# A depthwise convolution of the last pair of images on TensorE instead of VectorE, and some products of the late scans on GpSimd

## The chip, the cores and the metric

The kernel runs on one core of a Trainium2 chip. A core has five engines that run side by side, each through its own fixed list of instructions: TensorE (PE in the profile, with its weight loads shown apart as PEld), VectorE (DVE), ScalarE (ACT), GpSimd (POOL) and SyncE (SP), which here only issues DMA transfers. Operands lie in SBUF, and matmul results in the eight banks of PSUM. The metric is the device time of one execution in microseconds, given as the median of several runs.

## The reference

A network of two layers on x of shape (8, 256, 32, 32) in float32, that is eight images of 1024 tokens with 256 channels. Cut to what matters:

```python
# layer 0: a selective state space block, then a mixture of experts
h  = layernorm_over_channels(x)                     # (B, L=1024, 256)
xs, z = split(h @ W_in)                             # 512 channels each
xs = silu(causal_conv4(xs) + conv_b)
dt, Bm, Cm = parts(xs @ W_x)                        # dt through W_dt and softplus
for t in range(L):                                  # 16 states per channel
    hst = exp(dt[t] * A) * hst + dt[t] * xs[t] * Bm[t]
    y[t] = sum_over_states(hst * Cm[t])
x = x + ((y + xs * Dp) * silu(z)) @ W_out
x = x + sum over the 2 best of 8 experts of p_e * (gelu(x @ W1_e + b1_e) @ W2_e + b2_e)

# layer 1: an inception-like convolution, then a feed-forward of chosen tokens
v = layernorm_over_channels(x)                      # 256 channels in five parts:
#   128 unchanged | 32: 3x3 depthwise | 32: 1x11 depthwise | 32: 11x1 depthwise
#   | 32: a small state space block (64 channels, 16 states), as in layer 0
x = x + concat(parts)
w = layernorm(x) @ wr                               # rank the tokens of an image
x = x + feed_forward(256 -> 1024 -> 256, tanh-gelu) for the 511 best of 1024 tokens
```

## The kernel before

**Units and groups.** Layer 0's state space block is done in 16 *units*, each half an image (512 tokens). A unit has `norm`, `project`, `rows_of`, `dt_of` and `scan_unit`; the scans are 2 channel blocks x 8 pairs of states x 2 halves of the block, called *scan pairs* (two states at once). What follows is done in four *groups*, a pair of images each (n = 0 to 3; "pair 3" is the last): `route`, `scatter` with `put` (tokens go to slots of experts by indirect DMA), `experts` (23 blocks of 128 slots or fewer), `combine` (the outputs of the experts are gathered into the buffers `ys` and weighted), `taps_of` (the depthwise convolutions), `mamba_in`, `mamba_scan`, `mamba_out`, `assemble`, `ranks`, a second `put`, `feed_forward` in eight halves, and `finish`.

**One scan pair** (`scan_pair`), with the lines of the profile: GpSimd writes `dbu` = dtx * B for two states (line 801, 128 x 1024); ScalarE writes exp(dt * A) to a PSUM bank of the pool `mm` (line 806, once for each state); VectorE scans along the tokens, writing the states over that bank (line 809), and multiplies them by C, writing over `dbu` (line 812). TensorE then sums over the states by multiplying with an identity matrix into the PSUM tile `y` (as transposes in the units, line 793; as matmuls of 512 columns in the groups, line 830). In some pairs GpSimd first adds the two products (line 820), and TensorE has one summand instead of two. `PAIRED[i]` says for how many of the eight pairs of states of unit or group i this is so. When the state of a first half is needed by the second, a ScalarE copy keeps it (line 816). `end_y` closes a scan with a VectorE product of `y` with the gate (line 876). There are six `dbu` buffers, and four late in the kernel.

**The depthwise convolutions** (`taps_of`) of a pair of images read two padded images in SBUF, `pad_a` (128 partitions: the 3x3 and the 1x11 parts of both images, 17 shifts) and `pad_b` (64 partitions: the 11x1 part, 11 shifts). The first shift of each is a ScalarE instruction with scale and bias (line 1406), every other one a VectorE multiply-and-add of 1024 columns with one scale per partition (line 1408), on an accumulator in SBUF. So there are 28 shifts or *taps* for each pair of images, 26 of them on VectorE.

**The small state space block.** `mamba_in` turns the tokens (VectorE transposes of line 1422), projects and convolves them (TensorE, line 1462) and makes delta and dtx (line 773); `mamba_scan` has 8 pairs of states x 2 images = 16 scan pairs.

**The rest that is spoken of.** In `experts` and `feed_forward` the matmuls are those of lines 1219 (`hidden`) and 1241 (`second`). `combine` gathers by GpSimd's indirect DMA into two `ys` buffers (line 1317) and weighs by VectorE (lines 1335 and 1338). `ranks` counts by VectorE how many tokens of an image rank above each (lines 1618, 1623 and 1629). `put` is an indirect DMA too (line 1130), as is the gather of `finish` (line 1705). Line 1322 makes small diagonal matrices on ScalarE.

**The order.** No engine chooses at run time. Every piece of work is a `step` with an engine, an estimate of its duration, a priority and the buffers it reads and writes; `Flow.run` simulates the engines with these estimates and writes down one fixed order for each of them. The priorities come from a plan written by hand or tuned: `UNIT_AT` (when the scans of each unit begin), `PLAN` (one row for each group: where each of its parts begins, and the spacing of its pieces), and `KNOB` (how the choice weighs waits and buffers). For the matmuls of 128 x 512 in float32 that sum in the groups the steps say 0.9 us:

```python
step(PE, (0.48 if turned else 0.9) * (1 if paired else 2), prio + 2.5, sums, [dbu], [y], scan=True)
```

## Time and profile before

| | |
|---|---|
| median of 3 runs | 3333.59 us (3333.14 to 3346.01) |
| the profiled execution, its own time | 3336.01 us |
| its span in the profile | 3334.2 us |
| mean granted TensorE clock | 0.958 of full speed |
| TensorE busy | 2939.6 us (88%), weight loads 2009.1 us (60%) |
| VectorE busy | 2833.6 us (85%) |
| ScalarE busy | 2317.7 us (70%) |
| GpSimd busy | 2298.9 us (69%) |
| mean DMA rate | 203 GB/s |

The span is what the profile's timeline covers; the rest of the execution's own time lies around it. Busy shares are means over stages with different limits: up to 2452 us the units and the groups of earlier pairs are interleaved, after that the last pair of images goes through its parts one after another, with the remaining work of pair 2 beside it. A row of the groups of instructions reads: line, engine, operation, output <- inputs, shapes, count, then total busy us and the mean ns of one, then the idle time of the engine just before these instructions, and what ended most of it.

### The profile page before, as it was taken

How to read it: one execution, taken by the hardware profiler on the slowest of the kernel's cores; microseconds unless marked ns; L12 is line 12 of the kernel's file. 1: busy time of each engine (PE TensorE's matmuls, PEld its weight loads, DVE VectorE, ACT ScalarE, POOL GpSimd, SP SyncE). 2: the span in 40 equal slices, each digit the busy share in tenths (PEclk: the TensorE clock that was granted, in tenths of full speed). 3: DMA queues.
4: the chain of work that ended last, by engine and by line, in shares of the span. 5: the costliest groups of instructions: out<-in, count | busy, mean ns of one | idle time of the engine just before them, and what ended most of it. 6: DMA issues, size and time to landing. Idle time of an engine off the chain costs nothing. (4 is left out here: it accounts for less than half of the span.)

```text
span 3334.2 us, 43327 instructions
## 1 busy us (share of the span) xinstructions
PE 2939.6 (88%) x13348; PEld 2009.1 (60%) x13348; DVE 2833.6 (85%) x3924; ACT 2317.7 (70%) x4290; POOL 2298.9 (69%) x1650
## 2 busy tenths in 40 slices
PE   8888887888898989999999999898898889989948
PEld 4454554555656666666676664666766557865636
DVE  3999999999989998999998998968997889768841
ACT  5566776567878878988877876777856666557523
POOL 4678677688899969887776886785728764166331
PEclk9998999899999999999999999999998999999979
DMA  7343443345646556765555776666748787877745
GB/s 253 135 148 130 139 140 131 123 159 181 217 161 210 183 193 223 244 201 174 192 198 185 234 234 228 204 209 208 237 150 306 253 316 270 264 261 263 242 160 160
DMA packets 276709, 676.99 MB, mean 203 GB/s; under 512 B 31015, under 2 KB 115629, under 8 KB 276478
## 3 DMA queue, kind: packets, MB, share of 16 engines
q1 hardware_dynamic: 258046, 623.87, 56.0%
q0 software_dynamic: 18432, 50.36, 4.6%
q8 instruction: 107, 1.75, 0.2%
q14 instruction: 124, 1.02, 0.1%
HBM read 572.92 MB, written 101.19 MB: 202 GB/s over the span
## 5 line engine op out<-in xcount | busy, mean ns | idle before, releaser
L801 POOL TENSOR_TENSOR dbu<-dtx,bc 128x1024 f32<-128x1024 f32 x547 | 1291.2, 2375 | 236.2 <-DMA bc<-rows 109.2
L806 ACT ACTIVATE mm<-dt,neg_a 128x512 f32<-128x512 f32 x1152 | 771.3, 688 | 138.8 <-DVE dbu L812 121.8
L812 DVE TENSOR_TENSOR dbu<-mm,bc 128x512 f32<-128x512 f32 x1108 | 765.4, 691 | 50.7 <-DMA bc<-rows 1.4
L809 DVE TENSOR_TENSOR_SCAN mm<-mm,dbu 128x512 f32<-128x512 f32 x566 | 691.6, 1222 | 95.5 <-ACT mm L806 53.1
L809 DVE TENSOR_TENSOR_SCAN mm<-mm,state,dbu 128x512 f32<-128x512 f32 x562 | 720.7, 1282 | 21.8 <-ACT mm L806 15.3
L793 PE MATMUL y<-ident,dbu 128*128 128x128 f32 x3768 | 547.4, 286 | 183.6 <-DVE dbu L812 95.2
L793 PEld LDWEIGHTS y<-ident,dbu 128*128 128x128 f32 x3768 | 444.7, 146 | 367.8 <-POOL dbu L820 115.7
L1219 PE MATMUL mm<-xbt,we 128*128 128x256 f32 x1584 | 378.0, 390 | 11.3 <-ACT xbt L1207 3.5
L1241 PE MATMUL mm<-we,hid 128*128 128x256 f32 x1552 | 368.6, 387 | 13.3 <-ACT hid L1225 7.0
L1219 PEld LDWEIGHTS mm<-xbt,we 128*128 128x128 f32 x1584 | 304.2, 196 | 69.4 <-issue 10.6
L1241 PEld LDWEIGHTS mm<-we,hid 128*128 128x128 f32 x1552 | 290.1, 193 | 80.5 <-issue 20.6
L820 POOL TENSOR_TENSOR dbu<-dbu 128x512 f32<-128x512 f32 x174 | 227.0, 1305 | 119.4 <-DVE dbu L812 109.8
L816 ACT COPY state<-mm 128x1 f32<-128x1 f32 x576 | 90.0, 159 | 282.4 <-DVE dbu L812 272.6
L534 PE MATMUL y<-still 128*128 128x512 bf16 x1062 | 278.7, 397 | 0.0
L436 ACT ACT_TABLE_LOAD x198 | 254.0, 1283 | 3.7
L728 PE MATMUL mm<-pre,w_tap 128*128 128x512 f32 (+3 forms) x512 | 233.8, 598 | 7.2 <-ACT pre L716 6.0
L1225 ACT ACTIVATE hid<-mm,we 128x256 f32<-128x256 f32 x396 | 157.2, 475 | 35.5 <-PE mm L1219 20.1
L534 PEld LDWEIGHTS <-still 128*128 128x128 bf16 x1062 | 107.5, 102 | 110.5 <-issue 32.2
L1317 POOL DMA_INDIRECT ys<-slots_y,slot x128 | 127.1, 993 | 63.8 <-issue 26.0
L1705 POOL DMA_INDIRECT ys<-y,slot_t x64 | 64.8, 1013 | 153.7 <-DMA y<-xo 74.2
L728 PEld LDWEIGHTS mm<-pre,w_tap 128*128 128x128 f32 x512 | 92.4, 189 | 110.7 <-issue 93.9
L1130 POOL DMA_INDIRECT slots_x<-xg,slot x116 | 115.7, 997 | 39.9 <-issue 22.1
(289 smaller groups left out, 4661.4 us busy)
## 6 DMA issues: line engine op xcount, KB each, us to landing
bc<-rows SPq DMA_DIRECT2D x606, 512.0 KB
we<-in_W SPq DMA_DIRECT2D x81, 514.0 KB
we<-in_W SPq DMA_DIRECT2D x76, 512.0 KB
xb<-slots_x SPq DMA_DIRECT2D x92, 256.0 KB
slots_y<-xo SPq DMA_DIRECT2D x92, 256.0 KB
xc<-x SPq DMA_DIRECT2D x64, 256.0 KB
we<-in_W12f SPq DMA_DIRECT2D x21, 512.0 KB
slots_x<-xg SPq DMA_DIRECT2D x10, 1024.0 KB
```

The source lines that it names most:

```text
L436: nc.scalar.preload_act_table_set(tables[name])
L534: nc.tensor.matmul(live[0].v[:, 0], still, wide, start=False, stop=False)
L728: nc.tensor.matmul(tc_.v[:, cut:], w_tap[:, c, j], pre.v[:, cut + j : j + N], start=j == 3, stop=j == 0)
L793: nc.tensor.matmul(y.v[:, n, k * P : (k + 1) * P], src[:, k * P : (k + 1) * P], g.ident, start=start and k == 0, stop=stop and k == N // P ...
L801: gpsimd(2.38, prio, lambda: nc.gpsimd.tensor_tensor(dbu.v, dtxs.v[:, n : n + 1].to_broadcast(wide2), bt.v, ALU.mult), [dtxs, bt], [dbu], ...
L806: step(ACT, 0.69, prio, lambda j=j, h=h: nc.scalar.activation(h.v, dts.v[:, n], AF.Exp, scale=scales(j)), [dts], [h], table="exp", scan=True)
L809: step(DVE, 1.29 if at else 1.24, prio, lambda j=j, h=h: nc.vector.tensor_tensor_scan(h.v, h.v, dbu.v[:, j], 0.0 if initial is None else i ...
L812: product = step(DVE, 0.69, prio, lambda j=j, h=h: nc.vector.tensor_tensor(dbu.v[:, j], h.v, ct.v[:, j], ALU.mult), [h, ct], [dbu], scan=True)
L820: gpsimd(1.27, prio + 2.3, lambda: nc.gpsimd.tensor_tensor(dbu.v[:, 0], dbu.v[:, 0], dbu.v[:, 1], ALU.add), [], [dbu])
L1219: nc.tensor.matmul(tv[:, f], we[0].v[:, at : at + P], xbt.v[:, k], start=k == 0, stop=k == KC - 1)
L1225: nc.scalar.activation(hid.v[:, f], tv[:, f % 2], func, bias=we[0].v[:, at : at + 1])
L1241: nc.tensor.matmul(to, hid.v[:, f, h * P : (h + 1) * P], we[1].v[:, f * C : (f + 1) * C], start=extra is None and f == 0, stop=f == FC - 1,)
```

## The change

1. `taps_of` of pair 3 (n at or above `PE_TAPS` = 3) becomes TensorE work: every tap is a matmul with a diagonal matrix that holds the tap's weights, two halves of 512 columns each, summed in a PSUM bank (17 matmuls a half for `pad_a`, 11 for `pad_b`, 56 in all), in steps of four matmuls. ScalarE adds the bias and moves each half to the accumulator (4 instructions). The 26 VectorE and 2 ScalarE tap instructions of pair 3 are gone; pairs 0 to 2 keep theirs.
2. The 28 diagonal matrices are made by ScalarE (`spread_taps`, identity scaled per partition) in the SBUF places of the weights `w_pre`, `w_z` and `w_tap`, after the last `project` of layer 0 has read them.
3. A third kind of scan pair (`way` 2, a new list `HELD`): the scan writes the states over `dbu` in SBUF instead of over the PSUM bank, and GpSimd multiplies both by C in one instruction of 128 x 1024; TensorE sums two summands. It is used for 1 of 16 scan pairs in the small block of pair 1, 2 of 16 of pair 2, and 8 of 16 of pair 3.
4. `PAIRED` has other numbers: 180 added pairs in the units instead of 140, 24 in the groups instead of 38.
5. `UNIT_AT`, `PLAN` and `KNOB` have other numbers, so that the order of the other work moves too.

VectorE has 26 taps (104 to 78) and 22 products by C (1152 to 1130) less; GpSimd has 11 products by C more and 204 added pairs instead of 178. The number of transfers that SyncE issues is the same.

```diff
-PAIRED = [0, 3, 0, 2, 0, 0, 7, 6, 4, 0, 1, 0, 0, 5, 4, 3, 5, 5, 7, 2]
+PAIRED = [0, 4, 6, 4, 0, 1, 7, 2, 0, 2, 2, 0, 2, 5, 5, 5, 5, 1, 7, 1]
+HELD = [0, 0, 0, 0, 0, 0, 0, 0, 0, 0, 0, 0, 0, 0, 0, 0, 0, 1, 2, 8]
-UNIT_AT = [13, 52, 84, 119, 151, 183, 212, 243, 272, 303, 335, 367, 399, 430, 484, 522]
+UNIT_AT = [13, 56, 87, 118, 150, 183, 212, 242, 273, 304, 335, 367, 399, 430, 484, 522]
 PLAN = [
...
-    dict(put=4.35, experts=(475.48, 5.13), combine=(531.8, 1.84), taps=(660.36, 4.99), mamba=607.2, assemble=(658.29, 21.36), ranks=726.99, ffn=(887.16, 13.4), finish=(1263.31, 3.88)),
-    dict(put=8.79, experts=(589.95, 1), combine=(560.3, 13.52), taps=(748.92, 14.82), mamba=705.93, assemble=(727.02, 4.16), ranks=770.82, ffn=(1019.15, 1.97), finish=(1226.33, 0.05)),
+    dict(put=5.38, experts=(475.47, 5.12), combine=(521.25, 1.33), taps=(808.33, 6.52), mamba=613.73, assemble=(682.87, 25.29), ranks=744.51, ffn=(960.78, 5.51), finish=(1163.97, 13.06)),
+    dict(put=6.66, experts=(606.01, 1.74), combine=(783.79, 8.25), taps=(813.44, 7.71), mamba=683.76, assemble=(688.24, 0.97), ranks=770.96, ffn=(997.48, 5.59), finish=(1332.62, 0.63)),
 ]
+PE_TAPS = 3
-KNOB = [0.35, 0.14, 0.68, 0.65, 0, 1.38, 562.08]
+KNOB = [0.35, 0.13, 0.66, 0.63, 0, 1.4, 437.89]
...
+    def way_of(i, k):
+        def share(n, k, of):
+            return (k + 1) * n // of > k * n // of
+        return 2 if share(HELD[i], k, DS) else 1 if share(PAIRED[i], k // 2, DS // 2) else 0
...
+            step(DVE, us, prio, lambda j=j, h=h: nc.vector.tensor_tensor_scan(
+                dbu.v[:, j], h.v, dbu.v[:, j], 0.0 if initial is None else initial[1](j), ALU.mult, ALU.add),
+                [h, *at], [dbu], scan=True, ways=(2,))
...
+        if last is not None:
+            step(ACT, 0.17, prio + 1, lambda: nc.scalar.copy(
+                last[2](), dbu.v[:, :, N - 1 :]), [dbu], fills=[last[0]], ways=(2,))
+        gpsimd(2.38, prio + 1, lambda: nc.gpsimd.tensor_tensor(
+            dbu.v, dbu.v, ct.v, ALU.mult), [ct], [dbu], ways=(2,))
...
+    def tap_matrices():
+        places = [w_pre[:, k, c * P : (c + 1) * P] for k in range(KC) for c in range(NC0)]
+        places += [w_z[:, k, c * P : (c + 1) * P] for k in range(KC) for c in range(NC0)]
+        places += [w_tap[:, c, j] for c in range(NC0) for j in range(4)]
+        return [places[: len(TAPS_A)], places[len(TAPS_A) : len(TAPS_A) + len(TAPS_B)]]
...
+    def spread_taps(prio):
+        made = buf("token")
+        diagonals.append(made)
+        for k, (taps, scale, m) in enumerate([(TAPS_A, taps_a, P), (TAPS_B, taps_b, DI1)]):
+            for i in range(len(taps)):
+                step(ACT, 0.3, prio + 0.1 * i, lambda k=k, i=i, scale=scale, m=m: nc.scalar.activation(
+                    tap_matrices()[k][i][:m, :m], g.ident[:m, :m], AF.Copy, scale=scale[:, i : i + 1]),
+                    fills=[made]).needs.update(projections)
...
+            for hf in range(2 if n >= PE_TAPS else 0):
+                (t,) = banks()
+                for first in range(0, len(taps), 4):
+                    some = range(first, min(first + 4, len(taps)))
+                    now = prio + each * (first + hf + k * len(TAPS_A))
+                    def go(some=some, t=t, k=k, m=m, taps=taps, hf=hf, window=window):
+                        for i in some:
+                            nc.tensor.matmul(
+                                t.v[:m].rearrange("p (h w) -> p h w", w=32), tap_matrices()[k][i][:m, :m],
+                                window(*taps[i], top=16 * hf, high=16), start=i == 0, stop=i == len(taps) - 1,
+                            )
+                    step(PE, 0.45 * len(some), now, go, [at, *diagonals], [t], claims=[acc])
+                step(ACT, 0.62, prio + each * (len(taps) + hf + k * len(TAPS_A)), lambda t=t, acc=acc, scale=scale, m=m, taps=taps, hf=hf:
+                    nc.scalar.activation(
+                        acc.v[:m, 16 * hf : 16 * hf + 16], t.v[:m].rearrange("p (h w) -> p h w", w=32), AF.Identity,
+                        bias=scale[:, len(taps) :]), [t], fills=[acc])
...
         end = s + 2 * DS
         tokens(i, end + 1)
+        if i + 1 == len(units):
+            spread_taps(end + 2)
```

## The prediction, made before the changed kernel had run

> **What bounds the kernel now.** I read the page first, then stretches cut at the kernel's own joints, then the timelines of the joints.
>
> ```profile
> span 3334.2 us, 43327 instructions
> PE 2939.6 (88%) x13348; PEld 2009.1 (60%) x13348; DVE 2833.6 (85%) x3924; ACT 2317.7 (70%) x4290; POOL 2298.9 (69%) x1650
> ```
>
> No engine is full over the span, so the stages decide. The sixteen units of layer 0 end with the VectorE product of line 876 at 2452. Until then (busy shares between one such product and the next) VectorE is 84 to 97% busy in nearly every half unit. After it comes one long chain for the last pair of images (pair 3): route, scatter, experts, combine, convolution and mamba, assembly, ranks, feed-forward, finish. The stretches of that chain, with columns PE, PEld, DVE, ACT, POOL (busy us), granted clock, DMA share, GB/s:
>
> ```profile
> 2452.00:2691.00 239.00, 212.26 (x806) 140.57 (x804) 195.75 (x368) 147.28 (x282) 158.28 (x172) 0.92 0.72 240
> 2809.00:2921.00 112.00, 110.61 (x565) 95.38 (x564) 87.84 (x272) 53.15 (x117) 13.23 (x24) 1.00 0.78 247
> 2921.00:3005.00 84.00, 68.70 (x303) 49.72 (x302) 50.75 (x170) 45.99 (x94) 52.95 (x69) 0.95 0.80 262
> 3005.00:3053.00 48.00, 45.24 (x157) 24.48 (x155) 39.35 (x30) 37.74 (x59) 30.47 (x24) 0.98 0.68 227
> 3053.00:3129.00 76.00, 67.14 (x230) 41.07 (x231) 74.69 (x79) 46.72 (x86) 46.97 (x26) 0.93 0.83 290
> 3129.00:3204.00 75.00, 50.19 (x245) 37.86 (x243) 56.99 (x218) 23.51 (x50) 5.85 (x6) 0.87 0.42 134
> ```
>
> The reader should see four limits: 2809 to 2921 belongs to TensorE (experts, 110.6 of 112 us); 2921 to 3005 (combine of pair 3) to no engine; 3053 to 3129 (scans of pair 3) to VectorE (74.7 of 76); what follows is serial. In the combine stage it is a ring of gathers through two ys buffers, as the waits from 2460 to 3010 show:
>
> ```profile
> POOL ys L1317 <- DVE xo L1338: 20.5, 14, 5.2
> DVE xo L1338 <- DMA ys<-slots_y,slot: 17.8, 14, 3.2
> DVE xo L1335 <- DMA ys<-slots_y,slot: 16.2, 10, 3.9
> ```
>
> Eight blocks take 2936.9 to 3000.8, 8 us each, with VectorE at 60%. The timelines around the start of the last scans:
>
> ```profile
> 3018.98 15.80 DVE L1408 SCALAR_TENSOR_TENSOR dbu<-pad_a,taps_a,dbu 128x1024 f32<-128x1024 f32 x12
> 3039.97 13.24 DVE L1408 SCALAR_TENSOR_TENSOR dbu<-pad_b,taps_b,dbu 64x1024 f32<-64x1024 f32 x4
> 3053.14 1.21 DVE L809 TENSOR_TENSOR_SCAN mm<-mm,dbu 128x512 f32<-128x512 f32 x1
> 3042.35 3.21 POOL L773 TENSOR_TENSOR dtx<-dt,xs 128x1024 f32<-128x1024 f32 x1
> 3016.71 7.14 PE L1462 MATMUL mm<-xn,w_tap 64*128 64x512 f32 x16 [0.21 <-DVE xn L1447]
> ```
>
> Two thirds of the taps run while mamba_in(3) is still on its way to the first scan (3005 to 3048): VectorE would be idle there. And four taps take 13.24 us beside GpSimd, 3.31 each, against 1.32 (15.80/12) without.
>
> **The change part by part.** (1) Off VectorE for pair 3: 26 taps. By the rows above 16 cost 1.3 and ten cost 1.3 to 3.3, together 43 us. Of these only what stands in the scan stage is on the path: B taps until 3053.1, where the first dbu was ready at 3048.8 (4.3 us), two between scans (1.95 + 1.27), and those at 3125.8, which mostly wait beside GpSimd and the end anyway. So 7 to 10 us of 43, unless other work moves into the vacated 3005 to 3048. It does: in the new order both rank passes of pair 2 (36 us, from 2907 on before, the second among the first combine blocks) stand between mamba_in(3) and the first scan. The first pass came from a stretch where TensorE was the limit (110.6 of 112), so moving it gains nothing there; the second held up combine: its first product came at 2936.9, though its gathers were issued at 2926.9 to 2931.7 and take some 3 us to land. I take 4 us there, and 1 us for pair 2's puts no longer between the gathers; bounds 0 and 12. The ring of 8 us a block stays.
>
> (2) On TensorE: 28 taps x 2 halves = 56 matmuls of 512 columns. The nearest row is line 1462: 16 records are 8 such matmuls in 7.14 us, 0.89 each; taken at 0.87 for long runs, 49 us. The Trainium skill (TensorE: Matmul & The Clock Gate, section "Wait — 56ns, not 53.3ns?") gives warm matmuls a spacing of N/2.4 GHz plus about 2.5 ns, 0.216 us for 512 columns; with two records to a matmul the 56 would take 24 us, close to the 0.45 us each that the new step declares. The row has 0.446 us for one record, twice that, in f32. The measured one decides: 25 us more on TensorE than the order was laid out for. It matters, since only in this stage does TensorE get this work: in the order, 20 matmuls stand before the first sums of y and 36 among them. They also hold two of the mm banks at a time, which feed-forward would use; its two halves there are the ones that wait.
>
> (3) The scan stage of pair 3 summed by engine. T is the transpose of line 1422 (3004.9); before, the first scan is at T+48.2 and the product of line 876 that closes the stage at T+124.5. After: GpSimd's three leading products fall from 3.0-3.2 to 2.4 without taps beside them (-2), B taps no longer precede the first scan (-4), four tap matmuls stand ahead of the second delta matmul (+1.5, net of a feed-forward pass that stood there before): first scan near T+44. VectorE from there: 8 ordinary pairs x (2x1.25+2x0.69) + 8 held x 2x1.28 + 4 of other work = 55 us, so T+99. GpSimd from T+40: 16x2.36 + 8x2.36 held + an add 1.3 + puts and gathers 6 = 64, so T+105. TensorE: in order, behind the second delta matmul (T+31): 48 tap matmuls still to come 42, sums of y 31x0.87 = 27, two feed-forward halves (16 matmuls each, 7.1 by lines 1219 and 1241) and small ones 17: 86 us, so T+117, plus 2 to 4 for waits on sums and for the tap results holding two of the dbu buffers: T+119 to T+121. TensorE replaces VectorE as the limit here; gain about 4 us instead of 20. Five feed-forward halves of group 2 left this stage (35 us), or it would be longer.
>
> (4) Held C products. No row has a scan writing SBUF. From below: 1.22, as the PSUM form; from above 3.3, if it were blocked like the taps. The skill (SBUF — State Buffer, "Who interferes with whom") says a VectorE instruction with at most one SBUF input does not contend with GpSimd, and one with two does. This scan reads h from PSUM and dbu from SBUF, like the present one, whose mean is 1.22 to 1.28 beside a GpSimd that is 69% busy. I take 1.28; at 3.3 it would be 22x2 = +44 on VectorE. For the product on GpSimd I take line 801's 2.36, same shape; bounds 2.34 and 3.3. It waits for both scans of its pair; queued behind it in GpSimd's order are the dbu products of the pairs after next and puts of pair 2, and TensorE's sums wait for it, 2.4 us later than for a VectorE product. One or two dbu products run ahead of it in the order, so scans do not see it unless GpSimd is the limit.
>
> (5) Matrices: 28 ACT copies; nearest row line 1322, 0.39 us: 11 us during unit 15, where ACT is 73% busy and only the exps of the scans queue behind. Zero; uncovered at most 11, and 3 is what I keep for the range. State copies fall by a handful. SP issues as many DMAs as before.
>
> (6) PAIRED: 204 instead of 178 adds of 1.3 us; in the units 180 instead of 140: +52 us GpSimd, and 160 transposes fewer, -17 us TensorE. Unit 2 gets 24 (31 us): its GpSimd share goes from 0.65-0.78 to 0.9-0.97; units 7 to 9 lose 32. Half units with GpSimd at 0.88 or more had VectorE at 0.91 in the mean, the others before 2002 at 0.94: 2 us of 65 each. By GpSimd's work in the new order some ten half units are so crowded, nine before. Net 0, bounds -8 and +10.
>
> (7) Tail. All eight feed-forward halves of pair 2 now stand behind the last scan, four before: 28 us more TensorE in 3129 to 3204 and the next stretch, where it has 25 + 17 idle. GpSimd's puts for pair 3 still start behind one gather of pair 2, which needs the product behind ranks, as before (ranks end 3203.7, put 3209.8). So 0, bounds -5 and +8; 28 if TensorE's cover were gone.
>
> Sum: 0 (units) -5 (until T) -4 (scans) +0 (tail) = -9 on the profiled execution's 3336.0, hence 3327; the median of the runs shown is 2.4 lower, and I forecast 3326.
>
> **The rivals.** *Full gain:* the VectorE time is worth its length: 42 us of taps and 15 of products (22x0.69) come off a chain that was VectorE-bound. For it: 74.7 of 76 us. Against it: only 16 of these pairs' stage is so bound. Needs TensorE to keep pace; then T+105 rather than T+120, and with 10 us in the combine it gives -25 to -40: about 3303. *Slower, by TensorE in the last scans:* the sums of y stand behind eight-matmul tap groups (7 us each), the dbu buffers are freed late, GpSimd waits for them, scans wait for it. Price: at the granted 0.93 of that stretch 86 us become 92, and a wait of 2.5 us at each of eight pairs adds 20: T+142, and feed-forward of pair 2 is pushed into ranks and puts for another 5 to 10. +10 to +30: about 3352. It decides once the last sum comes later than T+125. *Not doing what it says:* that the order moves nothing off the path (ranks fill every gap, combine's ring stays at 8 us): -2 to +5, part of the likeliest.
>
> **How the numbers follow.** Likeliest case 0.43 (own range 3310 to 3340), full gain 0.34, slower 0.23. A measurement here can tell about 0.5% (17 us) from no change. Below 3317: 0.31 of the full gain and 0.09 of the likeliest: 0.40. Above 3350: 0.20 of the slower case and 0.02 of the likeliest: 0.22. Between: 0.38. Range 3296 to 3356, leaving out a tenth at either end: the full gain with its last 10 us of combine, and the slower case beyond its middle.
>
> **What would show it.** Line 1454's matmuls at 0.43 per record (0.21 would favour the full gain); the scan stage with PE at 95% and VectorE under 80%; first scan at T+44, last product near T+120; combine still 8 us a block; line 820's scans at 1.2 to 1.3; a GpSimd-crowded unit 2. I am wrong if T itself moves by more than 12 us, if the units' end moves from 2452 by more than 10, or if the last scans end before T+110 or after T+130.

## The result and the profile after

The changed kernel takes 3366.09 us (median of 8 runs, 3360.15 to 3374.7) against 3342.05 us for the kernel before (8 runs, 3333.14 to 3352.21, the three shown ahead among them): a ratio of 1.0074, 95% interval 1.0057 to 1.0092. It is slower by about 24 us where some 9 us less had been forecast. The page of the profiled execution:

```profile
span 3365.0 us, 43189 instructions
...
PE 2980.5 (89%) x13300; PEld 2024.6 (60%) x13300; DVE 2775.1 (82%) x3876; ACT 2309.9 (69%) x4312; POOL 2345.8 (70%) x1693
```

Against the page before, VectorE has 58.5 us less (2775.1 against 2833.6), GpSimd 46.9 more, TensorE 40.9 more, and the span is 30.8 longer. So VectorE was relieved as planned, and the kernel still became slower. The same stretches of the changed kernel, cut at the same events (columns PE, PEld, DVE, ACT, POOL busy us, granted clock, DMA share, GB/s):

```profile
2470.00:2714.00 244.00, 213.46 (x824) 141.25 (x822) 199.27 (x373) 146.98 (x283) 150.10 (x168) 0.95 0.72 240
...
2852.00:2944.00 92.00, 87.86 (x434) 74.86 (x433) 67.47 (x183) 37.91 (x86) 13.31 (x24) 0.98 0.67 214
2944.00:3024.00 80.00, 66.46 (x290) 48.89 (x288) 39.39 (x119) 45.66 (x97) 44.54 (x58) 0.94 0.83 270
3024.00:3069.00 45.00, 44.86 (x139) 21.50 (x138) 40.80 (x144) 25.15 (x39) 12.90 (x8) 1.00 0.41 136
3069.00:3145.00 76.00, 75.47 (x213) 34.66 (x212) 56.47 (x57) 36.88 (x75) 59.19 (x32) 1.00 0.70 225
3145.00:3231.00 86.00, 72.85 (x328) 51.14 (x327) 55.24 (x214) 30.82 (x63) 18.81 (x29) 0.94 0.66 210
```

The stage of the last scans (3069 to 3145) has TensorE at 75.5 of 76 us and VectorE at 56.5; before (the row 3053 to 3129 of the prediction) it was 67.1 and 74.7. The stretch ahead of it (3024 to 3069) is a TensorE stretch too, and VectorE is busy there for 40.8 of 45 us, mostly with pair 2's ranks. Set side by side, with T the first transpose of mamba_in(3):

| stretch, from the two profiled executions | before | after | difference |
|---|---|---|---|
| start to the last unit's gate product | 2452.4 | 2470.4 | +18.0 |
| units' end to T | 552.5 | 553.9 | +1.4 |
| T to the first scan of pair 3 | 48.2 | 45.2 | -3.0 |
| first scan to the gate product that closes the stage | 76.3 | 75.9 | -0.4 |
| that product to the end of ranks(3) | 74.3 | 85.9 | +11.6 |
| ranks(3) to the end | 130.5 | 133.7 | +3.2 |
| sum | 3334.2 | 3365.0 | +30.8 |

The profiled execution before was among the fastest of its kernel, so these differences add up to nearly 7 more than the medians show. The middle, where the change sits, is as forecast. The loss is at both ends, in work that the taps and the held scans hardly touch: 18 us in the units and 15 in the tail.

**The units.** VectorE's totals until the units' end, before and then after:

```profile
0.00:2453.70 2453.70, 2181.04 (x10196) 1474.71 (x10196) 2204.89 (x2603) 1829.55 (x3351) 1878.88 (x1235) 0.97 0.57 188
```
```profile
0.00:2471.70 2471.70, 2182.05 (x10049) 1472.76 (x10049) 2209.51 (x2603) 1833.03 (x3380) 1930.91 (x1276) 0.96 0.56 187
```

The same 2603 VectorE instructions, 4.6 us more busy; the other 13 us are idle time. VectorE's waits at the scans, by what ended them (us in total, times, longest), before and then after:

```profile
DVE mm L809 <- ACT mm L806: 66.5, 52, 4.5
DVE mm L809 <- POOL dbu L801: 27.1, 13, 5.5
```
```profile
DVE mm L823 <- ACT mm L818: 81.0, 54, 8.1
DVE mm L823 <- POOL dbu L811: 25.5, 16, 5.8
```

The waits for ScalarE's exponentials grew by 14.5 us, those for GpSimd's `dbu` did not grow. The scans that start from a state show the most of it:

```profile
L809 DVE TENSOR_TENSOR_SCAN mm<-mm,state,dbu 128x512 f32<-128x512 f32 x522 | 669.5, 1283 | 20.6 <-ACT mm L806 14.2 <-POOL dbu L801 6.2
```
```profile
L823 DVE TENSOR_TENSOR_SCAN mm<-mm,state,dbu 128x512 f32<-128x512 f32 x522 | 669.5, 1283 | 45.7 <-ACT mm L818 27.5 <-POOL dbu L811 12.7 <-issue 5.2
```

The figure behind the second bar is the idle time just before them: 20.6 us became 45.7, while the other rows of VectorE together have 12 us less. One profile could be chance; but in the changed kernel and the seven below with the same order in the units (e1, f4, f4b, f6, f9, f10, f11) these end between 2461.5 and 2476.8, and in the four kernels with the order of before (before, f1, f2, f8) between 2443.1 and 2455.7. The waits for exponentials agree: 79.7 to 86.8 us in the changed kernel, f4, f9, f10 and f11, against 61.0 to 68.5 in those four.

**The tail.** VectorE around the close of the scans, after:

```profile
3145.42 1.29 DVE L897 TENSOR_TENSOR sz<-sz,y 128x512 f32<-128x512 f32 x2 [1.80 <-PE y L850]
...
3148.96 1.24 DVE L1591 STREAM_TRANSPOSE dbu<-sq 64x1024 f32<-64x1024 f32 x1
...
3156.90 0.48 DVE L1780 SCALAR_TENSOR_TENSOR xc<-ys,tok,xc 128x256 f32<-128x256 f32 x1 [4.62 <-remote]
3158.48 0.48 DVE L1780 SCALAR_TENSOR_TENSOR xc<-ys,tok,xc 128x256 f32<-128x256 f32 x1 [1.10 <-DMA ys<-y,slot_t]
3158.88 0.42 DVE L1616 TENSOR_TENSOR xc<-mm,xc 128x256 f32<-128x256 f32 x1
...
3173.44 0.42 DVE L1616 TENSOR_TENSOR xc<-mm,xc 128x256 f32<-128x256 f32 x1 [7.38 <-PE mm L1610]
...
3183.26 0.42 DVE L1616 TENSOR_TENSOR xc<-mm,xc 128x256 f32<-128x256 f32 x1 [5.34 <-DMA xc<-x]
```

And before, where line 876 closes the scans and line 1551 is the assembly:

```profile
3113.02 0.87 DVE L1715 SCALAR_TENSOR_TENSOR xc<-ys,tok,xc 128x256 f32<-128x256 f32 x2
...
3129.44 1.28 DVE L876 TENSOR_TENSOR sz<-sz,y 128x512 f32<-128x512 f32 x2
...
3140.68 0.43 DVE L1551 TENSOR_TENSOR xc<-mm,xc 128x256 f32<-128x256 f32 x1 [5.04 <-DMA xc<-x]
```

In the changed kernel line 897 closes the scans. The first product of pair 3's assembly (line 1616) comes 13.5 us later, right behind the last product of pair 1's finish (line 1780); two later ones wait 7.4 and 5.3 us for their TensorE transposes and their loads. It ends 48.3 us after the close. Before, that finish had its last products at 3113 (line 1715), ahead of the close; the assembly began 11.3 us after the close and ended 37.0 after it. What stands in between is older work: from 3143 to 3158 GpSimd issues eleven gathers and puts of pairs 1 and 2, and the loads for them stand between the assembly's own in SyncE's list. The reason seems to lie upstream (f9 below tests it). Pair 2's ranks ran at 2907 to 2961 and now run in the gap before the first scan (3026 to 3069); so its puts, at 2969 to 3030 before, run at 3082 to 3104 and 3149 to 3177, behind GpSimd's work for the scans, and its eight feed-forward halves after them (3177 to 3259).

### The profile page after: what moved, and what is told of

It is laid out like the page before. It is cut to its first block, busy times and chain, and to the rows that moved or that the text cites. A ratio compares the mean times of both kernels' runs of the same rounds, so it can differ in the third digit from the quotient of the medians.

```text
span 3365.0 us, 43189 instructions
## 1 busy us (share of the span) xinstructions
PE 2980.5 (89%) x13300; PEld 2024.6 (60%) x13300; DVE 2775.1 (82%) x3876; ACT 2309.9 (69%) x4312; POOL 2345.8 (70%) x1693
## 5 line engine op out<-in xcount | busy, mean ns | idle before, releaser
L811 POOL TENSOR_TENSOR dbu<-dtx,bc 128x1024 f32<-128x1024 f32 x553 | 1306.3, 2376 | 217.0 <-DMA bc<-rows 96.4
L826 DVE TENSOR_TENSOR dbu<-mm,bc 128x512 f32<-128x512 f32 x1084 | 749.0, 691 | 47.4 <-DVE mm L823 0.5
L823 DVE TENSOR_TENSOR_SCAN mm<-mm,state,dbu 128x512 f32<-128x512 f32 x542 | 695.1, 1282 | 48.0 <-ACT mm L818 27.7
L802 PE MATMUL y<-ident,dbu 128*128 128x128 f32 x3620 | 524.6, 286 | 193.2 <-POOL dbu L840 108.7
L802 PEld LDWEIGHTS y<-ident,dbu 128*128 128x128 f32 x3620 | 428.5, 146 | 369.2 <-POOL dbu L840 162.7
L840 POOL TENSOR_TENSOR dbu<-dbu 128x512 f32<-128x512 f32 x197 | 254.2, 1291 | 107.1 <-DVE dbu L826 101.3
L539 PE MATMUL y<-still 128*128 128x512 bf16 x1042 | 270.9, 394 | 0.0
L1153 POOL DMA_INDIRECT slots_t<-xg,slot_t x44 | 45.7, 1039 | 137.0 <-ACT xg L1728 127.1
```

The costliest lines, as they stand in the source:

```text
L539: nc.tensor.matmul(live[0].v[:, 0], still, wide, start=False, stop=False)
L802: nc.tensor.matmul(y.v[:, n, k * P : (k + 1) * P], src[:, k * P : (k + 1) * P], g.ident, start=start and k == 0, stop=stop and k == N // P ...
L811: gpsimd(2.38, prio, lambda: nc.gpsimd.tensor_tensor(dbu.v, dtxs.v[:, n : n + 1].to_broadcast(wide2), bt.v, ALU.mult), [dtxs, bt], [dbu], ...
L823: step(DVE, us, prio, lambda j=j, h=h: nc.vector.tensor_tensor_scan(h.v, h.v, dbu.v[:, j], 0.0 if initial is None else initial[1](j), ALU. ...
L826: product = step(DVE, 0.69, prio, lambda j=j, h=h: nc.vector.tensor_tensor(dbu.v[:, j], h.v, ct.v[:, j], ALU.mult), [h, ct], [dbu], scan=T ...
L840: gpsimd(1.27, prio + 2.3, lambda: nc.gpsimd.tensor_tensor(dbu.v[:, 0], dbu.v[:, 0], dbu.v[:, 1], ALU.add), [], [dbu], ways=(1,))
```

## The experiments

Two kinds. In the first the lists are edited and the scheduler makes a new order. In the second the order of one kernel's steps is written down, and the edited kernel replays it, so that only the named steps differ (a step whose buffer is not free yet moves back to the first place where it is). `rank` below is a step's place in that list. The replay, in place of the scheduler's choice:

```python
todo = sorted(self.steps, key=lambda s: (rank[s.key], s.n))
while todo:
    for n, s in enumerate(todo[:400]):
        at = earliest(s) if not s.waits else None
        if at is not None:
            break
    del todo[n]
    ...
```

The diffs below are shortened to the steps that they name. Ratios are to the kernel before, with 95% intervals; stage times are from one profile each.

### New orders: parts undone, or alone

```diff
# e1_taps_vector, from after
-PE_TAPS = 3
+PE_TAPS = 4
# e2_units_as_before, from after
-PAIRED = [0, 4, 6, 4, 0, 1, 7, 2, 0, 2, 2, 0, 2, 5, 5, 5, 5, 1, 7, 1]
+PAIRED = [0, 3, 0, 2, 0, 0, 7, 6, 4, 0, 1, 0, 0, 5, 4, 3, 5, 1, 7, 1]
# e4_change_alone, from after: also UNIT_AT, PLAN and KNOB as before
-PAIRED = [0, 4, 6, 4, 0, 1, 7, 2, 0, 2, 2, 0, 2, 5, 5, 5, 5, 1, 7, 1]
+PAIRED = [0, 3, 0, 2, 0, 0, 7, 6, 4, 0, 1, 0, 0, 5, 4, 3, 5, 5, 7, 2]
# b1_pairs_alone, from before
-PAIRED = [0, 3, 0, 2, 0, 0, 7, 6, 4, 0, 1, 0, 0, 5, 4, 3, 5, 5, 7, 2]
+PAIRED = [0, 4, 6, 4, 0, 1, 7, 2, 0, 2, 2, 0, 2, 5, 5, 5, 5, 5, 7, 2]
```

> The changed kernel with the taps of pair 3 back on VectorE (PE_TAPS 4); the new PAIRED, HELD, UNIT_AT, PLAN and KNOB stay. Theory A (the loss is in the order: more added pairs on GpSimd in the units, and work of pairs 1 and 2 left behind the last scan): undoing the taps brings nothing back, units end again near 2470, time 3360 to 3378. Theory B (the 56 matmuls of 0.87 us are too much for TensorE late in the kernel): time falls to 3340 to 3350, the scan stage of pair 3 no longer ends on TensorE, and the tail from the last end_y to the end is back near 205 us.

> The changed kernel with the sixteen unit entries of PAIRED as before (140 added pairs in the units instead of 180). The order puts no puts of pair 2 behind the last scan here, and one gather of pair 1's finish where the changed kernel has eight tiles of them. Theory A: units end at 2450 to 2460 instead of 2470, tail back to 203 to 208 us, time 3332 to 3348. If the added pairs are free (as the prediction had it) the units still end near 2470 and only the tail is shorter: 3348 to 3355. Theory B: no change, 3360 to 3370.

> The two new mechanisms alone: taps of pair 3 as matmuls and the held scans (HELD as in the changed kernel), with PAIRED, UNIT_AT, PLAN and KNOB as before. Theory A: units end near 2452, scan stage of pair 3 at T+119 to T+122, no work of pairs 1 and 2 but the usual gathers in the tail: 3328 to 3344, 0 to 12 faster than before. Theory B: 3352 to 3368, the scan stage later than T+124.5.

> The kernel before with only the sixteen unit entries of PAIRED from the changed kernel (52 us more of adds on GpSimd in the units, 17 us less of transposes on TensorE). Theory A: units end at 2462 to 2472, time 3350 to 3362. If the adds are free: units end at 2452 within 4, time within 6 of before.

| run | us | ratio | units' end | first scan | close | close to end |
|---|---|---|---|---|---|---|
| e1_taps_vector | 3388.31 | 1.0131 [1.0109, 1.0154] | 2470.5 | T+45.1 | T+121.5 | 241.2 |
| e2_units_as_before | 3501.92 | 1.0471 [1.0447, 1.0495] | 2562.1 | T+54.8 | T+132.8 | 207.9 |
| e4_change_alone | 3368.52 | 1.0079 [1.006, 1.0098] | 2445.1 | T+53.6 | T+138.0 | 204.3 |
| b1_pairs_alone | 3470.37 | 1.0389 [1.0367, 1.0411] | 2502.9 | T+45.5 | T+124.0 | 243.2 |

In e1, e2 and b1 neither theory's time came true. Fewer adds on GpSimd cost 136 us against the changed kernel, more adds 125 against the one before, and e1 loses 22 us in a tail that its new order made, with the same time from T to the close: a list that was planned together with others is worth little apart from them, and such runs measure the new order rather than the edit. e4 is the useful one, and agrees with its theory B (half a microsecond above its range). With the plan of before the units end at 2445 and the tail is 204 us, so neither loss of the changed kernel is there. Instead T comes 574.8 us after the units' end (552.5 before), 18 of these 22 us already at the first gather of the combine, ahead of all tap matmuls; and from T to the close it takes 13.5 us longer. Its two stretches from T to the close:

```profile
3020.00:3073.50 53.50, 53.50 (x143) 23.69 (x142) 5.18 (x7) 26.75 (x40) 11.35 (x11) 1.00 0.39 135
3073.50:3158.00 84.50, 81.17 (x239) 40.58 (x238) 61.88 (x59) 40.40 (x77) 63.96 (x34) 0.94 0.74 238
```

TensorE is busy without a break to the first scan, 26 us of it tap matmuls; VectorE has 5.2 us to do. So with the plan of before the last scans close near where the prediction's rival of a slower kernel had them (T+142), and the new plan avoids that and loses in the units and the tail. The larger part of e4's loss lies ahead of the taps, and what makes it was not traced.

### Kept orders: the taps

```diff
# f1_taps_kept_order: order of before (pairs 560 to 575 are pair 3's scan pairs; j = 0 to 15)
-PE_TAPS = 4
+PE_TAPS = 3
+rank[f"taps_ofPE{j + 1}"] = rank[f"scan_pair{560 + j}POOL1"] + 0.3
# f6_taps_vector_kept: order of after (n = 0 to 25)
-PE_TAPS = 3
+PE_TAPS = 4
+rank[f"taps_ofDVE{79 + n}"] = rank[f"scan_pair{560 + n * 16 // 26}DVE2"] + 0.2 + 0.01 * n
# f8_column_taps_only: order of before (n = 0 to 5)
-            for hf in range(2 if n >= PE_TAPS else 0):
+            for hf in range(2 if n >= PE_TAPS and k == 1 else 0):
+rank[f"taps_ofPE{n + 1}"] = rank[f"scan_pair{561 + 2 * n}POOL1"] + 0.3
```

> The kernel before with its order of steps written down and kept; only the taps of pair 3 become matmuls (16 groups, one after each scan pair's dbu from the first scan pair on; a step whose PSUM bank is not free yet waits for it in the list), and the 28 matrices are made in unit 15. No held scans, PAIRED as before. Theory A (in this order TensorE has no room for them: 101 us of its own work from T to the close of the scan stage, plus 49): the stage closes at T+145 to T+152 instead of T+124.5 and the time is 3358 to 3375. Rival (the matmuls take the place of TensorE's idle time and warm-up matmuls, and VectorE's relief counts): the stage closes by T+126, time 3330 to 3345.

> The changed kernel with its order kept, but pair 3's 26 taps back on VectorE (and 2 on ScalarE), spread over its sixteen scan pairs; no matmul taps, no matrices made. In this order the ranks of pair 2 fill VectorE between T and the first scan, so the taps fall into the scan stage, which has VectorE at 56.5 of 76 us: it closes at T+140 to T+150 instead of T+121, TensorE drops to 45 of 76, time 3385 to 3400. Rival (the taps fit beside the scans, since TensorE is relieved of 53 us): within T+118 to T+126, time 3360 to 3370.

> The kernel before with its order kept; only the 11 taps of pad_b of pair 3 as matmuls (22 of them, 0.94 us each: 21 us for TensorE), the 16 of pad_a stay on VectorE, which loses 10 taps of 1.3 to 3.3 us. TensorE has 101 us of other work from T to the close: the stage closes at T+120 to T+127 against T+124.5, time 3336 to 3348: no gain to be told. Rival (VectorE's relief before the first scan and in the stage is the path): T+112 to T+118, time 3325 to 3334, faster than both kernels.

| run | us | ratio | first scan | close | close to end |
|---|---|---|---|---|---|
| f1_taps_kept_order | 3370.85 | 1.0093 [1.0074, 1.0112] | T+42.3 | T+156.1 | 206.6 |
| f6_taps_vector_kept | 3391.4 | 1.0144 [1.0123, 1.0164] | T+43.6 | T+153.8 | 215.7 |
| f8_column_taps_only | 3341.89 | 0.9993 [0.9981, 1.0005] | T+46.5 | T+130.5 | 205.4 |

The stretches from T to the first scan and on to the close, first of the order of before with the taps on TensorE, then of the order of after with them on VectorE:

```profile
3005.30:3047.60 42.30, 40.77 (x129) 21.28 (x127) 6.51 (x11) 31.37 (x50) 15.41 (x17) 0.93 0.59 195
3047.60:3161.40 113.80, 111.90 (x347) 57.95 (x347) 68.26 (x74) 53.40 (x97) 48.23 (x27) 1.00 0.59 207
```
```profile
3016.80:3060.40 43.60, 38.13 (x138) 19.84 (x136) 39.85 (x143) 26.75 (x39) 15.50 (x9) 0.96 0.46 150
3060.40:3170.60 110.20, 73.90 (x212) 31.75 (x211) 104.67 (x82) 34.49 (x70) 77.42 (x31) 0.86 0.46 150
```

The two are mirror images. In the first, TensorE is full (111.9 of 113.8) and VectorE has 68; in the second VectorE is full (104.7 of 110.2) and TensorE has 74. Each order has been filled up to its limit on the engine that the taps are moved to, so moving them alone closes the stage about 32 us later either way: in the order of before the taps on TensorE cost 31 us of time, in the order of after the taps on VectorE 25. Theory A of f1 and the first theory of f6 hold; both put the close some 4 us too early. f8 is smaller: 22 matmuls (20.1 us), no difference in time that can be told, and a stage that closes 6 us later, 3.5 beyond what was expected, not 6 to 12 sooner. How much of these 6 us is the taps' is open: TensorE's granted clock from T to the first scan was 0.84 in this execution, against 0.98 before.

### Kept orders: the held scans and the added pairs

```diff
# f2_held_kept_order: order of before; the GpSimd product stands where the second VectorE product stood
-HELD = [0] * 20
+HELD = [0, 0, 0, 0, 0, 0, 0, 0, 0, 0, 0, 0, 0, 0, 0, 0, 0, 1, 2, 8]
+rank[f"scan_pair{p}POOL2"] = rank[f"scan_pair{p}DVE4"] + 0.3
# f11_none_held: order of after; each VectorE product stands behind its scan
-HELD = [0, 0, 0, 0, 0, 0, 0, 0, 0, 0, 0, 0, 0, 0, 0, 0, 0, 1, 2, 8]
+HELD = [0] * 20
# f3_adds_kept_order: order of after; PAIRED of the units as before, 88 adds off, 48 other ones on
+rank[f"scan_pair{p}POOL2"] = rank[f"scan_pair{p}PE1"] - 0.5
# f3b_adds_off: order of after; the same 88 adds off, none on
+        if flow.pair in NOT_ADDED:
+            way = 0
```

> The kernel before with its order kept; only the held scans (1, 2 and 8 of 16 scan pairs of pairs 1, 2 and 3): scan over dbu, one GpSimd product by C in the place of the second VectorE product. Taps stay on VectorE. If the held scan costs the same 1.28 us and the product 2.4 us as the prediction took: VectorE loses 11 us of the 76 of the last stage, GpSimd gains 19 on 39: the stage closes 2 to 8 us earlier, time 3334 to 3343. Rival (the wait for both scans in GpSimd's order delays the next dbu): the stage closes 5 to 15 later, 3348 to 3360.

> The changed kernel with its order kept and no held scans: the 22 products by C go back to VectorE right behind their scans, and GpSimd loses 11 products of 2.37 us. VectorE goes from 56.5 to about 67 of 76 us in pair 3's scan stage, GpSimd from 59 to 40; TensorE stays at 75. If TensorE is the limit there, as the prediction has it: the stage closes within T+118 to T+124, time within 6 of the changed kernel. Rival (the held scans are what lets VectorE keep up): T+126 to T+132, time 3370 to 3378.

> The changed kernel with its order kept and the unit entries of PAIRED as before (140 added pairs in the units instead of 180; an add that is new here stands just before the sums of its pair). Theory A1 (the adds on GpSimd cost the 18 us by which the units end later): units end at 2450 to 2460, time 3346 to 3358. Theory A2 (the order of the other work costs them; the adds are about free): units end within 5 of 2470, time 3360 to 3371.

> The changed kernel with its order kept, and in the units that it gives more added pairs than before (88 pairs, 24 of them in unit 2) no GpSimd add: TensorE sums both products. Nothing is added elsewhere, so 92 added pairs are left in the units. Theory A1 (these adds cost the 18 us by which the units end later): units end at 2450 to 2460. Theory A2 (the order of the other work costs them): units end at 2465 to 2480, time 3360 to 3378.

| run | us | ratio | units' end | close |
|---|---|---|---|---|
| f2_held_kept_order | 3345.38 | 1.0011 [0.9999, 1.0022] | 2455.7 | T+134.6 |
| f11_none_held | 3365.23 | 1.0089 [1.0073, 1.0105] | 2468.9 | T+122.7 |
| f3_adds_kept_order | 3386.08 | 1.0138 [1.0117, 1.0159] | 2488.7 | T+121.1 |
| f3b_adds_off | 3362.04 | 1.0056 [1.0036, 1.0075] | 2465.9 | T+121.2 |

*Held scans.* f11 is level with the changed kernel, and the stage closes 1.6 us later although VectorE has 11 us more to do in it:

```profile
3066.00:3143.00 77.00, 77.00 (x224) 35.36 (x222) 67.84 (x71) 36.66 (x74) 41.06 (x23) 1.00 0.68 220
```

TensorE sets it, as the prediction had it. f2 is a miss between its two theories: 5 us slower than the kernel before by medians, its interval just touching no change. Of the 10 us by which its stage closes later, six come ahead of the first scan (54.5 us after T), where TensorE's granted clock was 0.84 in this execution against 0.98. In the stage itself 16 products were taken off VectorE, 11 us, and it is as busy as before (75.8 us against 74.9). The products of pair 1's finish, in the stage before and then with held scans:

```profile
L1715 DVE SCALAR_TENSOR_TENSOR xc<-ys,tok,xc 128x256 f32<-128x256 f32 x8 | 8.0, 1038 | 0.0
```
```profile
L2148 DVE SCALAR_TENSOR_TENSOR xc<-ys,tok,xc 128x256 f32<-128x256 f32 x8 | 18.2, 2309 | 0.0
L1188 DVE TENSOR_TENSOR_SCAN dbu<-mm,state,dbu 128x512 f32<-128x512 f32 x14 | 17.1, 1262 | 0.0
```

The same eight instructions took 18.2 us instead of 8.0. GpSimd had 62.6 of 80 us there against 46.9 of 76. The mean hides two kinds. Of the 64 such products in the whole trace of before, the 51 with no GpSimd product or add beside them took 0.46 to 0.49 us; twelve that began while one was running took 0.93 to 2.59 us and ended 0.28 or 0.29 us after the end of a GpSimd instruction. In f2 one took 8.32 us. The row merges it with the next, and the rows below are what GpSimd did meanwhile:

```profile
3093.34 8.71 DVE L2148 SCALAR_TENSOR_TENSOR xc<-ys,tok,xc 128x256 f32<-128x256 f32 x2
```
```profile
3093.21 2.35 POOL L1206 TENSOR_TENSOR dbu<-dbu,sz 128x1024 f32<-128x1024 f32 x1
3095.51 2.35 POOL L1179 TENSOR_TENSOR dbu<-dtx,bc 128x1024 f32<-128x1024 f32 x1
3097.82 1.26 POOL L1208 TENSOR_TENSOR dbu<-dbu 128x512 f32<-128x512 f32 x1
3099.04 2.33 POOL L1179 TENSOR_TENSOR xs<-dtx,bc 128x1024 f32<-128x1024 f32 x1
```

It outlasted four GpSimd instructions in a row; the product after it took 0.47 us. The held scans of f2 took 1.27 us on average beside a running GpSimd product or add, and 1.26 without one. The Trainium skill (SBUF — State Buffer, "Who interferes with whom") states that a VectorE instruction with two SBUF inputs contends with a GpSimd instruction that reads SBUF, and one with a single SBUF input does not; these rows agree with both halves: line 2148 reads ys and xc from SBUF, the scan reads h from PSUM. So in this order what the held scans took off VectorE came back on its neighbours.

*Added pairs.* f3b has 88 adds less on GpSimd (108.9 us less busy until the units' end) and its units end at 2465.9, inside the spread of that order. VectorE's waits for exponentials are 80.8 us there, as with the adds. Theory A2: the adds cost nothing that can be told, as step 6 of the prediction had it, and the 18 us are the order's. f3, the first try, was 20 us slower than the changed kernel, by its 48 new adds: the loss arises between 1010 and 1301 us, in units 7 and 8, to which most of those go, in an order that left no place for them. So adds are not free wherever they stand: with these 48 the units end 23 us later than in f3b.

### Kept orders: the tail

```diff
# f4_assembly_first and f4b_assembly_ranks: order of after
-        "tok": tiles("tok", [P, 8, 2 * NI, 1], 2),
+        "tok": tiles("tok", [P, 8, 2 * NI, 1], 3),
-        "slot_t": tiles("slot_t", [P, 2, 2 * NI], 2, dt=I32),
+        "slot_t": tiles("slot_t", [P, 2, 2 * NI], 3, dt=I32),
+rank[k] = rank["mamba_outDVE4"] + 0.001 * (n + 1)    # k: assembly(3); in f4b then ranks(3)
+rank[f"finish{e}{n}"] = rank["putPOOL192"] + ...     # f4: four tiles of finish(1); in f4b beside the ranks
# f9_pair2_earlier: order of after (k: ranks of pair 2; then its 16 puts)
+rank[k] = a + (b - a) * (n + 0.5) / len(keys)        # a, b: first product of combine(3), T
+rank[f"putPOOL{129 + 2 * n + m}"] = b + (c - b) * (n + 0.5) / 8 + 0.03    # c: dtx products of pair 3
# f10_half_ffn_pair2: order of after
-hid = hidden(xbt, we, AF.Gelu_apprx_tanh, line, now, "gelut")
+hid = hidden(xbt, we, AF.Gelu_apprx_tanh, line, now, "gelut", KC // 2 if n == 2 else KC)
-o, _ = second(hid, we, now, None if half else (ones[32:33], fb2))
+o, _ = second(hid, we, now, None if half else (ones[32:33], fb2), FC // 2 if n == 2 else FC)
```

> The changed kernel with its order kept but for the tail: the assembly of pair 3 stands ahead of everything else once mamba_out is done, the last four tiles of pair 1's finish are moved behind the second put of pair 3, and tok and slot_t have three buffers instead of two so that the assembly need not wait for them. Theory A (the tail is longer because the assembly of pair 3 waits for pair 1's finish, through the tok and xc buffers): VectorE's assembly ends 36 to 40 us after the last end_y instead of 48, time 3352 to 3360. Rival (the backlog on TensorE and the puts of pair 2 set the tail in any case): 3362 to 3370.

> As the run with the assembly of pair 3 first, and now its ranks too stand ahead of pair 2's feed-forward on ScalarE, VectorE and TensorE (there they had waited 31 us behind it), and the last four tiles of pair 1's finish go beside the ranks instead of behind the second put. tok and slot_t have three buffers. Theory A (the tail is 15 us longer because pair 1's finish and pair 2's puts stand before pair 3's assembly): ranks end 62 to 72 us after the last end_y instead of 86, and the time is 3345 to 3357. Rival (TensorE's backlog, pair 2's eight feed-forward halves, sets the end whatever the ranks do): ranks end early but the time stays at 3360 to 3372.

> The changed kernel with its order kept, but pair 2's last two assembly tiles and its ranks stand among pair 3's combine (as before the change) instead of between T and the first scan, and its sixteen puts stand between T and pair 3's dtx products, where GpSimd was 12.9 of 45 us busy, instead of behind the scans. Pair 2's feed-forward keeps its place. Theory A (the tail is 15 us longer because pair 2's puts and pair 1's last finish tiles run there ahead of pair 3's assembly and of pair 2's feed-forward): T moves by 0 to 8 later, the scan stage closes at T+115 to T+122, and the tail falls from 220 to 203 to 212: time 3350 to 3364. Rival (the feed-forward backlog alone sets the tail): tail 217 to 222, time 3366 to 3376.

> The changed kernel with its order kept; in pair 2's feed-forward half of each contraction is left out (hidden over one of two blocks of 128, second over half of its blocks), so that its eight halves take about 36 us of TensorE instead of 72; all transfers, activations and puts stay. If TensorE's backlog sets the longer tail: tail 200 to 210 instead of 220, time 3350 to 3358. Theory A (the waits for pair 1's finish and pair 2's puts set it): tail 214 to 221, time 3360 to 3368.

| run | us | ratio | units' end to T | close | close to: assembly's end | ranks' end | end |
|---|---|---|---|---|---|---|---|
| after | 3366.09 | 1.0074 [1.0057, 1.0092] | 553.9 | T+121.1 | 48.3 | 85.9 | 219.6 |
| f4_assembly_first | 3389.61 | 1.0141 [1.0119, 1.0163] | 552.3 | T+121.1 | 24.7 | 91.7 | 245.5 |
| f4b_assembly_ranks | 3406.95 | 1.0194 [1.0172, 1.0216] | 553.4 | T+121.0 | 24.4 | 65.6 | 258.6 |
| f9_pair2_earlier | 3375.15 | 1.0117 [1.0102, 1.0131] | 565.6 | T+126.8 | 42.8 | 79.6 | 207.3 |
| f10_half_ffn_pair2 | 3362.02 | 1.0077 [1.0063, 1.009] | 558.1 | T+121.2 | 48.0 | 84.8 | 214.6 |

f4 shows the wait: freed of pair 1's finish the assembly ends 24 us sooner. And it shows what comes next. The first step of ranks(3) is two small ScalarE instructions, which stood behind pair 2's feed-forward in ScalarE's list:

```profile
3195.88 0.18 DVE L2022 SCALAR_TENSOR_TENSOR tok<-tok 128x16 f32<-128x16 f32 x1 [31.10 <-ACT tok L2019]
```

The finish tiles that were moved behind the second put of pair 3 now hold up its feed-forward, which begins 154 us after the close instead of 126. f4b mends the wait of the ranks, which end 20 us sooner than in the changed kernel, as expected. The time is worse still: the rest of pair 1's finish, placed beside the ranks, now holds up the puts of pair 2 in GpSimd's list,

```profile
3191.71 0.95 POOL L2151 DMA_INDIRECT ys<-y,slot_t  x1 [37.81 <-DVE xc L2161]
```

so pair 2's feed-forward begins 80 us after the close instead of 31, and pair 3's second put, which has a gather of pair 2's finish in its midst, ends at 3314 instead of 3268. Both are misses on the time; the backlog is a chain of its own, and putting pair 3 ahead of it does not shorten it.

f9 takes the ranks and puts of pair 2 out of the way earlier, and the tail falls by 12 us to 207, near the 205 of before: theory A for the tail. But the same work costs 11.7 us between the units' end and T (the ranks among pair 3's combine) and 5.7 us from T to the close (puts ahead of the dtx products on GpSimd), which had been expected at 0 to 8 and at nothing, so the time is slower instead of faster. f10 takes about half of TensorE's work out of pair 2's feed-forward; its tail of 214.6 us lies among those of kernels of this order whose tail was not edited (214.0 in f11, 216.1 in f3b, 218.6 in f3, 219.6 in the changed kernel), and its time cannot be told from the changed kernel's. So of the 15 us most hang on where pair 2's ranks and puts stand, little on TensorE's backlog.

No version beat the kernel before: f8 and f2 cannot be told from it, and every other one is slower.

## Why the prediction was wrong

The time fell outside the range of 3296 to 3356, on its slow side. One of the signs that the prediction named came true: the units' end moved by 18 us, where it had allowed 10. Its last sum is a little off (3327 less 2.4 is 3324.6, not 3326), which changes nothing. Step by step:

1. *Taps off VectorE, before T (-5 forecast).* Measured +1.4 from the units' end to T, just outside its bounds of 0 to 12 of gain. From its first gather to its last block the combine was 5.1 us shorter, the size that was expected there, but otherwise made up: 1.9 us (4 expected) between the first gather and the first product, and 3.2 in the ring, 7.6 us a block where 8.0 was to stay. Its first gather came 5.1 us later relative to the units' end, and that took it back; the prediction had no term for it. That ranks of pair 2 would fill the gap after T was right (VectorE 40.8 of 45 us).
2. *56 matmuls at 0.87 us.* TensorE was busy 50.4 us with them, 0.90 each. The measured row was the right one to trust; the 0.45 us in the step and the 24 us from the warm spacing were not. The Trainium skill (FP8 and Floating Point Precision, "TensorE Precision Notes") gives true float32 four passes through the array; with the 0.216 us above, an estimate of 0.86 us, near what was measured.
3. *The scan stage.* First scan forecast at T+44, measured T+45.2; close T+119 to T+121, measured T+121.1; TensorE at 95% forecast, 99% measured; VectorE under 80%, 74%. This step held, in its mechanism too: TensorE replaced VectorE as the limit.
4. *Held scans.* 1.27 us against 1.28 taken, the product 2.36 to 2.37 against 2.36; worth nothing in the new order (f11), as the TensorE limit implied.
5. *Matrices.* 28 ScalarE copies, 10 us in unit 15; no effect was seen.
6. *PAIRED (0 forecast, -8 to +10).* The adds cost nothing that can be told (f3b), yet the units ended 18 us later. Here is the first failed step. It counted the adds and asked how crowded GpSimd would be; it took for granted that the rest of the units' order, with new UNIT_AT, PLAN and KNOB, was as good as the old one, and so put its cost at nothing. The price was in waits of the scans for ScalarE's exponentials, 81.0 us instead of 66.5.
7. *Tail (0 forecast, -5 to +8).* The second failed step, measured +15. The prediction saw that all of pair 2's feed-forward would stand behind the last scan, asked only whether TensorE had room for it, and booked the gain of the moved ranks in step 1 with no cost against it. It named the ranks' new place but did not follow what hangs on it: the puts of pair 2 behind GpSimd's scan work, then the feed-forward, and pair 1's finish ahead of pair 3's assembly. With ranks and puts earlier (f9) the tail is 207.3 us instead of 219.6, but 17.4 us are lost ahead of it.

Of the rivals, *full gain* fell with TensorE at 99%. *Slower, by TensorE in the last scans* has the size of the result but not its place: it is what e4 (T+138) and f1 (T+156) show, the mechanism without a plan made for it. In the changed kernel the plan had cleared TensorE for the taps, and the bill came where the cleared work went.

What exactly in the new order makes ScalarE's exponentials later in the units stays open: the time of the added pairs on GpSimd is excluded, but not that the scheduler, given them, ordered the rest differently. UNIT_AT, PLAN and KNOB were not tried one by one, since a PAIRED changed alone already made orders 125 us or more worse.

## What to carry to other kernels

Moving work from a full engine to another pays only if the other has room in that very stage; where it is made room for, follow the displaced work to its new place and through everything that waits for it (ranks, puts, feed-forward, finish), with each queue it is put behind. When a change comes with a re-planned order, price the order as a part of its own: here it lost 18 us in stages whose work had not changed, and one planned list changed alone cost 125 and 136 us. To measure a mechanism under such a scheduler, replay a fixed order and edit only the steps in question.

## What the hardware showed that was not expected

A VectorE product with two SBUF inputs that began while GpSimd was at a product or an add did not end before it: it ended 0.28 or 0.29 us after a GpSimd instruction had (twelve of twelve in before, twelve of twelve in f2), once after the fourth of four in a row (8.32 us instead of 0.48). With held scans on GpSimd this gave back ten of the eleven us that had been taken off VectorE (f2). GpSimd's share of the stage does not tell the price alone: 0.78 in f2 with a mean of 2.31 us, and also 0.78 in the changed kernel, where six such products took 1.10. How many GpSimd instructions follow each other without a break while the product waits does.

The granted clock of TensorE in the stretch from T to the first scan was between 0.84 and 1.00 in the profiles of these kernels. At 0.84 (f2) the first scan came 6 us later than at 0.98 (before), with nearly the same work ahead of it. This is one execution, and what set the clock was not looked into.
